# A two-layer graph network on one core: one tile of source rows in every fourth block as TensorE products in place of a gather

## The chip, the cores and the metric

The kernel runs on one NeuronCore of one Trainium2 chip. The metric is the device time of one execution in microseconds (us). TensorE, VectorE, ScalarE, GpSimd and SyncE appear in the profile as PE, DVE, ACT, POOL and SP; PEld is TensorE's weight load.

## The reference, cut to what matters

A graph has 6250 nodes of 128 features and 200,000 edges, sorted by destination. Two layers run one after the other, each with a residual sum.

```python
h = relu(layernorm(x))                        # layer 0: attention over edges, 8 heads of 16
z = h @ W;  el, er = z . attn_l, z . attn_r   # per node and head
e = leaky_relu(el[src] + er[dst])
a = exp(e - segment_max(e, dst)[dst])
x = x + segment_sum(z[src] * a, dst) / segment_sum(a, dst) + bias
h = relu(layernorm(x))                        # layer 1: messages weighted by a small network
s, v = h[:, :32] @ W_up_s, h[:, 32:] @ W_up_v # 128 numbers a node: the table of layer 1
w0, w1, w2, w3 = silu(silu(edge8 @ A1 + b1) @ A2 + b2) @ A3
m = [s[src]*y_s*w0, (v[src].y_v)*w3, s[src]*y_v*w1, v[src]*y_s*w2]   # 256 numbers an edge
x = x + (segment_sum(m, dst) / 10) @ W_out
```

Both layers need, for every edge, the row of its source node: 136 numbers in layer 0, 128 in layer 1.

## The kernel before, in words

**Tiles and blocks.** 128 edges make a tile, 1563 tiles in all, and 16 tiles (`KB`) make a block, 98 blocks (`NB`). As the edges are sorted, a block's destinations lie in a window of 128 nodes. `one_hot` (line 1146) compares a tile's destinations with `iota` and gives a 128x128 matrix `s`; the sum over edges is then a TensorE product of `s` and the messages, into `p_u`. `finish` (line 1154) joins the windows of adjacent blocks, and every second block completes one tile of 128 nodes, of which there are 50 (`NX`).

**Source rows.** Each layer first has its table in DRAM, `t0` or `t1`, one row a node. `gather` (line 831) issues one indirect DMA on GpSimd for each tile of 128 edges and brings 128 rows into one slot of the block's buffer `z` (name `g`). `z_pool` has five such buffers, so GpSimd can run ahead of the arithmetic. GpSimd does nothing else in the loops. In every third block (`by_row`, line 1106: 31 blocks) the last tile is left out of the gathers. `rows_by_row` (line 1117) has SyncE read 128 row addresses into registers and issue 128 row DMAs in place of it; `rows_until` spreads them over three blocks; `filled` (line 1142) has ScalarE copy the tile `r` into `z`.

**Layer 0** (the loop at line 1415) computes logits, maxima and weights of a block, multiplies and sums. For each complete node tile `node_x`, `node_d`, `node_h`, `node_t`, `node_s` compute the new x and the rows `sv` of the table of layer 1, and `node_out` (line 1343) has SyncE write `sv` to `t1` and to `t1z`. The second table lets the first 24 gathers (`NE`) of layer 1 begin before the last three node tiles (`NL`) are known: their rows are zero there, and `late_ends` and `late_rows` add them as f32 TensorE products with `sv_late`. All x lie in SBUF in `x_all`, 50 x 128 x 4 bytes a partition, from layer 0 until layer 1 ends.

**Layer 1** (the loop at line 1709) goes by steps of four tiles, four steps a block. At a block's first step `take_rows(b + 2)` asks for the gathers of the block after the next, and `edge_rows(b + 2)` has SyncE load edge data `ft` and `yb`. Each step then has, in this order: a quarter of the next block's `network` (TensorE products into `p_h`, ScalarE activations), `tensor_weights` of the next step (`p_w`), `messages` of this step (seven VectorE operations that read `z` and write `mj`), `one_hot` of the next step, `finish` and `node1` where a window is complete, and `sums1` (TensorE, from `mj` into `p_u`). `node1` (line 1625) transposes the sums, has ScalarE copy them, multiplies by `wout` and adds to x; `node_out1` has SyncE write the result one block later. PSUM's eight banks are full: two each of `p_h`, `p_w`, `p_u`, one `p_n`, and one `p_i` (called `held`), which keeps a copy of `iota` and the edge vectors `yp` of three blocks.

**Order.** TensorE, VectorE, ScalarE and SyncE run strictly in the written order (`manual_schedule`), and semaphores between engines follow from the tiles that are read and written. GpSimd's queue holds the gathers in their order. An engine that waits holds up all that is queued behind it on that engine.

A check of the data at the start picks this program or a general one that makes no use of windows. The profiled execution took this one.

Of the kernel before, what the change touches and what calls it, by code (L numbers as in the profile page):

```python
# [18 lines left out]
P = 128  # L19
# [10 lines left out]
KB = 16  # L30
# [711 lines left out]
def tile_even_edges(  # L742
# [88 lines left out]
    def gather(to, table, tiles, width, first=0):  # L831
        for k, t in enumerate(tiles, first):
            nc.gpsimd.indirect_dma_start(  # L833
                out=to[:, k, :width], out_offset=None, in_=table,
                in_offset=bass.IndirectOffsetOnAxis(ap=src_col[:, t : t + 1], axis=0))
        return to
# [171 lines left out]
def even_edges(tc, v):  # L1008
# [8 lines left out]
    with ExitStack() as ctx:  # L1017
        z_pool = ctx.enter_context(tc.tile_pool(name="fz", bufs=5))
        const = ctx.enter_context(tc.tile_pool(name="fconst", bufs=1))
        s_pool = ctx.enter_context(tc.tile_pool(name="fs", bufs=16))  # L1020
        row_pool = ctx.enter_context(tc.tile_pool(name="frow", bufs=3))
        of_l0 = ctx.enter_context(ExitStack())
        l0c = of_l0.enter_context(tc.tile_pool(name="l0c", bufs=1))
# [15 lines left out]
        x_all = const.tile([P, NX, P], F32, name="fx_all")  # L1039
# [3 lines left out]
        identb = l0c.tile([P, P], BF, name="fidentb")  # L1043
        nc.vector.tensor_copy(identb, ident)
# [50 lines left out]
        a3p = const.tile([P, 2, P], F32, name="fa3p")  # L1095
        nc.sync.dma_start(a3p, v["a3p"])
# [4 lines left out]
        wout = const.tile([P, 2, P], F32, name="fwout")  # L1101
        nc.sync.dma_start(wout, v["wout"])
# [43 lines left out]
        def one_hot(t, m, iota=iota):  # L1146

            s = s_pool.tile([P, 4, P], F32, name="s")
            nc.vector.tensor_tensor(s[:, :m], iota[:, None, :].to_broadcast([P, m, P]),  # L1149
                                    dloc[:, t : t + m].unsqueeze(2).to_broadcast([P, m, P]),  # L1150
                                    OP.is_equal)
            return s

        def finish(b, p_u, width, carry, agg, pool):
# [10 lines left out]
            return carry, agg  # L1165

# [5 lines left out]
        with tc.manual_schedule(engines=in_order), \  # L1172
# [116 lines left out]

            def node_rows(i, n):  # L1290
                nc.sync.dma_start(x_all[:, i : i + n, :],
                                  xp[i * P : (i + n) * P].rearrange("(j p) f -> p j f", p=P))

            def with_bias(i, n):
                x_i = x_all[:, i : i + n, :]
                nc.vector.tensor_add(x_i, x_i, bias_b[:, None, :].to_broadcast([P, n, F]))

            def node_x(u):
                i, n, agg = u["i"], u["n"], u["agg"]
                x_i = x_all[:, i : i + n, :]  # L1300
# [14 lines left out]
            def node_h(u):  # L1315
                i, n = u["i"], u["n"]
                rs, mr = normal(l0n, u["mv"], u["rs"], n, f"n{n}")
                xn = u["xn"] = l0n.tile([P, 2, P], F32, name="xn")
                nc.scalar.activation(xn[:, 0, :], x_all[:, i, :], AF.Identity, bias=mr[:, 0, :],
                                     scale=rs[:, 0, :])  # L1320
                if n == 2:
                    nc.vector.tensor_scalar(xn[:, 1, :], x_all[:, i + 1, :], u["mv"][:, 1, 0:1],
                                            rs[:, 1, :], op0=OP.subtract, op1=OP.mult)
# [19 lines left out]
            def node_out(u):  # L1343
                i, n, sv = u["i"], u["n"], u["sv"]
                first = i * P - W0
                for table in (t1, t1z) if i < LATE else (t1,):
                    if i == 0:
                        nc.sync.dma_start(table[: P - W0, :], sv[W0:, 0, :])
                    else:
                        nc.sync.dma_start(  # L1350
                            table[first : first + n * P].rearrange("(j p) f -> p j f", p=P), sv)

# [62 lines left out]
            for g in range(NG - 3):  # L1415
# [17 lines left out]
                maxima(c)  # L1433
                ends_of(n2, 1)
# [30 lines left out]
                ends_of(n2, 3)  # L1465
                for n in nodes:
                    node_s(n)
                late = nodes
                if b4:
                    sums(b4, 8)  # L1470
                if g == NG - 4:
# [16 lines left out]
            maxima(c3)  # L1488
            neighbours(c4, c5, c3)
# [26 lines left out]
            (u,) = ended(c4, st)  # L1516
            weighted(c2, 0)
# [22 lines left out]
        with tc.manual_schedule(engines=in_order), \  # L1540
                tc.tile_pool(name="l1", bufs=3) as l1, \
                tc.tile_pool(name="l1n", bufs=2) as l1n, \
                tc.tile_pool(name="l1_ps", bufs=2, space=PSUM) as l1_ps:

# [8 lines left out]
            def network(b, step):  # L1553
# [7 lines left out]
                if step == 3 or 2 * q0 + 8 >= KT[b] and second:  # L1561
                    c["yp"] = held[:, P + b % 3 * KB * 3 : P + (b % 3 + 1) * KB * 3].rearrange(
# [61 lines left out]

            def node1(i, agg):
                x_i = x_all[:, i, :]
                p_n = l1_ps.tile([P, 4, P], F32, name="p_n", bufs=1)
# [3 lines left out]
                nc.scalar.copy(m_t, p_n[:, :2])  # L1631
                for q in range(2):
                    nc.tensor.matmul(p_n[:, 2, :], m_t[:, q, :], wout[:, q, :], start=q == 0, stop=q == 1)
                nc.vector.scalar_tensor_tensor(x_i, p_n[:, 2, :], POST, x_i, op0=OP.mult, op1=OP.add)
                return i

            def node_out1(i):
                x_i = x_all[:, i, :]
                if i == 0:
                    nc.sync.dma_start(out[: P - W0, :], x_all[W0:, 0, :])  # L1640
# [5 lines left out]
            iota_p = held[:, :P]  # L1646
# [25 lines left out]
            def late_rows(t):  # L1672
                if t < NE:
                    z, k0, oh = blk[t // KB]["z"], t % KB, late_ends.of.pop(t)
                    p_n = l1_ps.tile([P, 4, P], F32, name="p_n", bufs=1)
                    for k in range(4):
                        for j in range(NL):
                            nc.tensor.matmul(p_n[:, k, :], oh[:, j, k, :], sv_late[:, j, :],
                                             start=j == 0, stop=j == NL - 1)
                    z = z[:, k0 : k0 + 4, :P]  # L1680
                    nc.vector.tensor_add(z, z, p_n)
# [6 lines left out]
            def take_rows(b):  # L1688
# [3 lines left out]
                elif b < NB:  # L1692
                    blk[b]["z"] = gathered(t1, range(b * KB, b * KB + KT[b] - (b in by_row)), P)

            rows, rows_until.n, late = rows_by_row(1, t1, P), 0, []
# [9 lines left out]
            us[0]["s"] = one_hot(0, us[0]["m"], iota_p)  # L1705
# [3 lines left out]
            for i, u in enumerate(us):  # L1709
                b, k0, m = u["b"], u["k0"], u["m"]  # L1710
                if k0 == 0:
                    take_rows(b + 2)
                    filled(1, b, blk[b]["z"], P)
                    edge_rows(b + 2)
                if k0 == 4:
# [8 lines left out]
                messages(u)  # L1724
                late_rows(4 * (i + 1))
                if i + 1 < NU:
                    n = us[i + 1]
                    n["s"] = one_hot(n["b"] * KB + n["k0"], n["m"], iota_p)
# [18 lines left out]
            p_n = l1_ps.tile([P, 4, P], F32, name="p_n", bufs=1)  # L1747
# [11 lines left out]
            x_i = x_all[:, NX - 2 :, :]  # L1759
# [140 lines left out]
```

## Time and profile before

| | us |
|---|---|
| median of 3 runs | 6222.33 (6202.72 to 6229.55) |
| the profiled execution's own time | 3867.0 |
| its span, first to last instruction | 3865.1 |
| layer 0 to layer 1, about | 1967 from the start |
| busy: GpSimd, TensorE, VectorE, ScalarE | 2900.2, 2825.6, 2237.5, 1403.0 |
| GpSimd gathers of lines 833 and 899 | 3064, a little under 1 us busy each |
| TensorE clock granted, layer 0 and layer 1 | 0.65, 0.97 |
| SyncE row DMAs | 7936, 0.5 KB each |

The runs are without a profile and take much longer than the execution that was profiled. Every duration below is from that one execution. In the lines of the profile, "L833" is a line of the kernel, "out<-in" are tile names, and the part after the bar gives the idle time of the engine just before and what ended it.

### The profile page before, as it was taken

The page shows a single profiled execution, that of the slowest core. Times are in us where ns is not written, and L with a number is a line of the kernel's source. Part 1 is how long each engine was busy: PE and PEld are TensorE (multiplying, and loading weights), DVE is VectorE, ACT ScalarE, POOL GpSimd, SP SyncE. Part 2 cuts the span into 40 slices and gives each one's busy share as a digit, 9 for nine tenths or more (in the row PEclk, how much of TensorE's full clock was granted, in tenths as well). Part 3 has the DMA queues.
Part 4 walks back from the last instruction along what each step waited for, and adds up shares of the span by engine and source line. Part 5 has one row for each costly group of instructions (what it writes and reads, how often), then busy time and mean ns, then how long its engine had stood idle before and what let it go on. Part 6 is the DMA issues. An engine that isn't in the chain of part 4 may idle for free. (4 is left out here: it accounts for less than half of the span.)

```text
span 3865.1 us, 62861 instructions
## 1 busy us (share of the span) xinstructions
PE 2825.6 (73%) x14836; PEld 2380.3 (62%) x14836; DVE 2237.5 (58%) x5485; ACT 1403.0 (36%) x3625; POOL 2900.2 (75%) x3074
## 2 busy tenths in 40 slices
PE   4666566666666666666688888888887788888777
PEld 3666566666566656656576666666665666666655
DVE  6555444444444444444457777777766666666666
ACT  3333322232323233322324444444444444444443
POOL 6777777777777777777777777777777777777776
PEclk7676666666666666666689999999999999999999
DMA  6222222222222222222222222222222222222221
GB/s 176 60 64 62 65 64 62 65 64 63 63 64 63 64 62 65 62 64 62 62 60 62 62 62 62 62 63 62 61 63 62 62 62 62 62 61 62 61 61 50
DMA packets 192048, 250.91 MB, mean 65 GB/s; under 512 B 78768, under 2 KB 141872, under 8 KB 191664
## 3 DMA queue, kind: packets, MB, share of 16 engines
q0 software_dynamic: 98048, 207.21, 22.6%
q1 hardware_dynamic: 93184, 39.50, 3.9%
q8 instruction: 120, 1.97, 0.2%
q14 instruction: 264, 2.16, 0.2%
q10 hardware_dynamic: 432, 0.08, 0.0%
HBM read 232.98 MB, written 13.25 MB: 64 GB/s over the span
## 5 line engine op out<-in xcount | busy, mean ns | idle before, releaser
L833 POOL DMA_INDIRECT g<-ft,fsrc x3024 | 2857.7, 945 | 934.4 <-issue 859.1
L1622 PE MATMUL p_u<-mj,s 128*128 128x256 f32 x3126 | 793.6, 398 | 211.2 <-DVE mj L1614 209.8
L1622 PEld LDWEIGHTS p_u<-mj,s 128*128 128x128 f32 x3126 | 591.1, 196 | 379.4 <-DVE mj L1614 303.3
L1286 PE MATMUL p_u<-g,s 128*128 128x136 f32 x3062 | 588.1, 372 | 1.0 <-DVE g L1281 0.4
L1286 PEld LDWEIGHTS p_u<-g,s 128*128 128x128 f32 x3062 | 563.2, 276 | 1.7 <-DVE g L1281 1.6
L1589 ACT ACTIVATE p_w<-p_w,yb 128x64 f32<-128x64 f32 x1563 | 450.3, 288 | 120.5 <-PE p_w L1585 78.8
L1605 DVE TENSOR_TENSOR vy<-g,p_i 128x384 f32<-128x384 f32 x387 | 213.0, 550 | 364.6 <-DMA g<-ft,fsrc 258.1
L1585 PE MATMUL p_w<-fa3p,h 128*128 128x256 f32 x1564 | 412.3, 387 | 0.0
L1203 PE MATMUL p_d<-fident,s 128*128 128x128 f32 x1563 | 370.6, 400 | 0.9 <-DVE s L1149 0.9
L1585 PEld LDWEIGHTS p_w<-fa3p,h 128*128 128x128 f32 x1564 | 289.3, 195 | 117.9 <-issue 51.9
L1228 DVE TENSOR_TENSOR e_s<-g,p_n 128x128 f32<-128x128 f32 x96 | 27.5, 286 | 554.6 <-DMA g<-ft,fsrc 498.1
L1570 ACT ACTIVATE h<-p_h,fb 128x512 f32<-128x512 f32 x196 | 134.7, 687 | 580.2 <-PE p_h L1568 580.2
L1203 PEld LDWEIGHTS p_d<-fident,s 128*128 128x128 f32 x1563 | 300.7, 218 | 11.6 <-DVE s L1149 1.1
L1196 ACT COPY mk<-p_m 128x385 f32<-128x385 f32 (+1 forms) x99 | 47.7, 482 | 701.4 <-PE p_m L1193 693.6
L1281 DVE TENSOR_TENSOR g<-g,pe 128x1024 f32<-128x1024 f32 x193 | 225.5, 1209 | 127.3 <-ACT g L1272 127.3
L1205 ACT CAST d<-p_d 128x512 bf16<-128x512 f32 x391 | 228.2, 586 | 180.4 <-PE p_d L1203 137.2
L1231 PE MATMUL pe<-fident,e_s 128*128 128x128 f32 x98 | 37.7, 384 | 329.9 <-DVE e_s L1229 329.9
L1149 DVE TENSOR_TENSOR s<-p_n,fdloc 128x512 f32<-128x512 f32 x391 | 266.1, 682 | 7.2 <-ACT sv L1341 3.4
L1149 DVE TENSOR_TENSOR s<-p_i,fdloc 128x512 f32<-128x512 f32 x391 | 266.4, 681 | 3.8 <-ACT p_i L1564 3.8
L1568 PE MATMUL p_h<-ft,fa1p 128*128 128x128 f32 x1568 | 215.4, 282 | 67.7 <-DMA ft<-in_e_f_dram 67.7
L1568 PEld LDWEIGHTS p_h<-ft,fa1p 128*128 128x128 f32 x1568 | 209.2, 196 | 88.6 <-issue 72.4
L1575 ACT ACTIVATE h<-p_h,fb 128x512 f32<-128x512 f32 x196 | 134.7, 687 | 304.4 <-PE p_h L1572 304.4
(213 smaller groups left out, 3345.6 us busy)
## 6 DMA issues: line engine op xcount, KB each, us to landing
r<-ft SPq DMA_DIRECT2D x3968, 0.5 KB
r<-ft SPq DMA_DIRECT2D x3968, 0.5 KB
g<-ft,fsrc POOLq DMA_INDIRECT x3024
ft<-in_e_f_dram SPq DMA_DIRECT2D x98, 64.0 KB
yb<-in_e_y_dram SPq DMA_DIRECT2D x98, 32.0 KB
fx_all<-in_e_xp_dram SPq DMA_DIRECT2D x48, 64.0 KB
out_dram<-fx_all SPq DMA_DIRECT2D x47, 64.0 KB
ft<-sv SPq DMA_DIRECT2D x46, 64.0 KB
```

What stands on the lines that cost most here:

```text
L833: nc.gpsimd.indirect_dma_start(out=to[:, k, :width], out_offset=None, in_=table, in_offset=bass.IndirectOffsetOnAxis(ap=src_col[:, t : t + ...
L1149: nc.vector.tensor_tensor(s[:, :m], iota[:, None, :].to_broadcast([P, m, P]), dloc[:, t : t + m].unsqueeze(2).to_broadcast([P, m, P]), OP. ...
L1203: nc.tensor.transpose(p_d[:, k, :], c["s"][q][:, k, :], ident)
L1205: nc.scalar.copy(d[:, :m], p_d[:, :m])
L1281: nc.vector.tensor_mul(zh, zh, p_a[:, k0 : k0 + m].unsqueeze(3).to_broadcast([P, m, H, D]))
L1286: nc.tensor.matmul(c["p_u"][:, :ZW], c["s"][k // 4][:, k % 4, :], c["z"][:, k, :], start=c["o"] + k == 0, stop=c["o"] + k == KT[c["b"]] - 1)
L1568: nc.tensor.matmul(p_h[:, q, :], a1p[:, q0 + q, :], c["ft"], start=True, stop=True)
L1570: nc.scalar.activation(c["h1"], p_h, AF.Silu, bias=b1)
L1585: nc.tensor.matmul(w[:, k : k + n].rearrange("p k a u -> p (k a u)"), c["h2"][q // 4][:, q % 4, :], a3p[:, :n].rearrange("p k f -> p (k f) ...
L1589: nc.scalar.activation(w[:, k, ::2, :], w[:, k, ::2, :], AF.Copy, scale=c["yb"][:, k0 + k, 0:1])
L1605: nc.vector.tensor_mul(vy, v_n, y_p)
L1622: nc.tensor.matmul(blk[b]["p_u"][:, :MW], u["s"][:, k, :], u["mj"][:, k, :], start=k0 + k == 0, stop=k0 + k == KT[b] - 1)
```

## The change

It concerns layer 1 and what layer 0 leaves behind for it.

- **Dense tiles.** In blocks 10, 14, ..., 90 (`dense1`, 21 blocks) tile 14 of 16 (`KD`) is not gathered. Its rows are made on TensorE: the table lies in SBUF as `t1s`, 50 node tiles in three bf16 parts whose sum is the f32 value. The node tiles are dealt into three ranges of 17 (`NR`). `dense_ends` spreads the edges' source numbers over the partitions with one f32 product and compares them with node numbers, which gives 17 one-hot matrices in bf16; `dense_rows` multiplies each with the three ranges' node tiles at once, 3 x 128 columns, for each of the three parts; `dense_taken` picks for each edge the range that it belongs to and writes the row into `z`. The steps of block b - 1 and of block b carry these (`dense_step`).
- **Parts.** In layer 0 `parts` splits each `sv` by two casts and two subtractions, and ScalarE's queue writes the parts to DRAM (`t1b`). Layer 1 loads them, six node tiles a block in its first eight blocks (`table_tiles`). The last three node tiles are split in SBUF.
- **x in DRAM.** `x_all` is gone. Layer 0 loads each node tile's x into a small buffer and ScalarE's queue writes the new x to `x1`; layer 1 loads it again (`node_rows1`).
- **Room.** `a3p` and `wout` are loaded at the start of layer 1; `one_hot` has a pool of 16 buffers in layer 0 and one of 5 in layer 1; `p_n` moves into the free half of the bank `held`, whose `yp` are now those of two blocks; its old bank becomes `p_x`, for `late_rows` and the dense tiles.

```diff
     def gather(to, table, tiles, width, first=0):
-        for k, t in enumerate(tiles, first):
+        for t in tiles:
+            k = first + t - tiles[0]
...
+        NR = -(-NX // 3)
+        KD = KB - 2
+        order = sorted(range(NR), key=lambda k: (k > 0, 2 * NR + k < NX, k))
+        half = (NR + 1) // 2
+        dense1 = set(range(10, NB - 4, 4))
...
+        def in_three(to, of, rest):
+            nc.vector.tensor_copy(to[:, :, 0, :], of)
+            nc.vector.tensor_sub(rest, of, to[:, :, 0, :])
+            nc.vector.tensor_copy(to[:, :, 1, :], rest)
+            nc.vector.tensor_sub(to[:, :, 2, :], rest, to[:, :, 1, :])
...
             def node_rows(i, n):
-                nc.sync.dma_start(x_all[:, i : i + n, :],
-                                  xp[i * P : (i + n) * P].rearrange("(j p) f -> p j f", p=P))
+                x_i = x_of[i] = l0n.tile([P, n, P], F32, name=f"x{n}", bufs=5 if n == 1 else 1)
+                nc.sync.dma_start(x_i, xp[i * P : (i + n) * P].rearrange("(j p) f -> p j f", p=P))
...
+                nc.scalar.dma_start(x1[i : i + n].rearrange("j p f -> p j f"), x_of.pop(i))
+
+            def parts(u):
+                i, n = u["i"], u["n"]
+                if i < LATE:
+                    u["parts"] = l0n.tile([P, 1, 3, P], BF, name="parts")
+                    in_three(u["parts"], u["sv"], l0n.tile([P, 1, P], F32, name="rest", bufs=1))
+
+            def parts_out(u):
+                if "parts" in u:
+                    nc.scalar.dma_start(t1b[u["i"]], u["parts"][:, 0])
...
+            def node_rows1(i, n=1):
+                x_i = x_of[i] = l1n.tile([P, n, P], F32, name=f"x{n}", bufs=4 if n == 1 else 1)
+                nc.sync.dma_start(x_i, x1[i : i + n].rearrange("j p f -> p j f"))
+
             def node1(i, agg):
-                x_i = x_all[:, i, :]
-                p_n = l1_ps.tile([P, 4, P], F32, name="p_n", bufs=1)
+                x_i = x_of[i][:, 0, :]
...
-            iota_p = held[:, :P]
+            iota_p, p_n = held[:, :P], held[:, 2 * P :].rearrange("p (j f) -> p j f", f=P)
...
+            def table_tiles(b):
+                i = 6 * b
+                if i < LATE:
+                    n = min(6, LATE - i)
+                    nc.sync.dma_start(t1s[:, i : i + n], t1b[i : i + n].rearrange("j p s f -> p j s f"))
+
+            def dense_ends(b):
+                p_x = blk[b]["p_x"] = l1_ps.tile([P, 4, P], F32, name="p_x", bufs=1)
+                nc.tensor.matmul(p_x[:, 3, :], key[:, b : b + 1].to_broadcast([P, P]), ident,
+                                 start=True, stop=True)
+                oh = blk[b]["oh"] = l1d.tile([P, NR, P], BF, name="ohs")
+                for k, n in ((0, half), (half, NR - half)):
+                    nc.vector.tensor_tensor(
+                        oh[:, k : k + n], p_x[:, 3:4, :].to_broadcast([P, n, P]),
+                        place_r[:, k : k + n].unsqueeze(2).to_broadcast([P, n, P]), OP.is_equal)
+
+            def dense_rows(b, k0, n):
+                c = blk[b]
+                for k in range(k0, min(k0 + n, NR)):
+                    i = order[k]
+                    m = len(range(i, NX, NR))
+                    for s in range(3):
+                        nc.tensor.matmul(c["p_x"][:, :m, :], c["oh"][:, k, :], t1s[:, i::NR, s, :],
+                                         start=k == 0 and s == 0, stop=k == NR - 1 and s == 2)
+
+            def dense_taken(b):
+                c = blk[b]
+                z = c["z"][:, KD, :P]
+                nc.vector.tensor_scalar(z, c["p_x"][:, 0, :], part[:, b, 0:1], None, op0=OP.mult)
+                for r in (1, 2):
+                    nc.vector.scalar_tensor_tensor(z, c["p_x"][:, r, :], part[:, b, r : r + 1], z,
+                                                   op0=OP.mult, op1=OP.add)
+
+            def dense_step(b, q):
+                if b + 1 in dense1:
+                    if q == 1:
+                        dense_ends(b + 1)
+                    elif q > 1:
+                        dense_rows(b + 1, (q - 2) * 4, 4)
+                if b in dense1:
+                    dense_rows(b, 8 + 3 * q, 3)
+                    if q == 2:
+                        dense_taken(b)
...
                     edge_rows(b + 2)
+                    if b % 2 == 0:
+                        node_rows1(b // 2, 1 if b < NB - 2 else 2)
+                    table_tiles(b)
...
                 messages(u)
+                if i == 26:
+                    in_three(t1s[:, LATE:], sv_late, rest)
+                dense_step(b, k0 // 4)
                 late_rows(4 * (i + 1))
```

## The prediction

> **What bounds the kernel now.** I read the page first, its line of engines, then its costliest group.
>
> ```profile
> span 3865.1 us, 62861 instructions
> PE 2825.6 (73%) x14836; PEld 2380.3 (62%) x14836; DVE 2237.5 (58%) x5485; ACT 1403.0 (36%) x3625; POOL 2900.2 (75%) x3074
> L833 POOL DMA_INDIRECT g<-ft,fsrc x3024 | 2857.7, 945 | 934.4 <-issue 859.1
> ```
>
> No engine looks full. But GpSimd's idle time is almost all "issue" (859.1 of 934.4 us): it waits for nothing that the profile shows. One gather is 945 ns busy plus some 300 ns of issue. Next, busy time by stretches for that line alone (columns: stretch, length, busy and count, TensorE clock, DMA share, GB/s).
>
> ```profile
> 500.00:1000.00 500.00, 378.00 (x401) 0.63 0.28 64
> 2500.00:3000.00 500.00, 377.98 (x401) 0.97 0.24 62
> ```
>
> It is the same count, 401 in 500 us, in the first layer and in the second: a pitch of 1.247 us that never breaks. GpSimd makes 3064 gathers in all (3024, and 40 in the smaller groups); 3064 x 1.247 = 3821 us of 3865. The two layers are one queue of gathers, and everything else follows it. Then the waits between 2100 and 3850 us, to see how closely the second layer follows (columns: total us, times, longest).
>
> ```profile
> DVE vy L1605 <- DMA g<-ft,fsrc: 257.1, 158, 3.7
> PE p_h L1568 <- DMA ft<-in_e_f_dram: 62.3, 25, 4.9
> ```
>
> VectorE waits for gathered rows, which is the proof from the consumer's side. The second line is a warning: TensorE also waits for edge data that SyncE loads. So I read SyncE's queue in order of time and VectorE's beside it.
>
> ```profile
> 2035.10 0.37 SPq L1549 DMA_DIRECT2D ft<-in_e_f_dram  x1
> ...
> 2383.53 0.37 SPq L1549 DMA_DIRECT2D ft<-in_e_f_dram  x1
> ```
>
> Between these two loads lie 19 blocks: 18.34 us a block, with SyncE issuing row after row and hardly waiting. GpSimd needs 15.67 gathers a block (one tile in every third block is SyncE's), 19.53 us. SyncE is therefore only 1.2 us a block from being a bound.
>
> ```profile
> 2032.06 0.55 DVE L1605 TENSOR_TENSOR vy<-g,p_i 128x384 f32<-128x384 f32 x1 [1.56 <-ACT p_i L1564]
> ...
> 2065.35 0.56 DVE L1605 TENSOR_TENSOR vy<-g,p_i 128x384 f32<-128x384 f32 x1 [1.20 <-ACT p_i L1564]
> ```
>
> These are the fourth steps of two blocks, two apart, at the start of the layer, while arithmetic is behind the gathers: 33.3 us for two blocks, 16.65 each. That is the fastest pace of the arithmetic that the trace shows. The order of pressure in the second layer is thus gathers 19.53, SyncE 18.34, arithmetic 16.65 us a block.
>
> **What the Trainium skill says.** "DMA: Bandwidth & Descriptors", section "SWDGE vs HWDGE vs iDMA": for a GpSimd DMA a GpSimd core computes each descriptor in software. That agrees with 945 ns for any 128 rows, while the DMA engines are 28% busy. "TensorE: Matmul & The Clock Gate", section "Back-to-back issue gap": a warm product of N columns takes about N/2.4 + 2.5 ns. Eight records of 128x256 f32 in the second layer take 1.89 us, so (1.89 - 0.38)/7 = 0.216 us each: twice 256 columns at that rate. The trace has no stream of bf16 products of 384 columns; by the page they are 0.162 us each. "SBUF — State Buffer", section "Who interferes with whom": a VectorE copy or cast can hold the port pair that GpSimd needs. Here 33 multiply-type VectorE operations of line 951 ran among the first 16 gathers and the gathers kept a median of 944 ns, with one of 1092.
>
> **The change, part by part.**
>
> *Removed: gathers.* Blocks 10, 14, ..., 90 are 21 blocks, each with one tile of 128 rows fewer. 21 x 1.247 = **26.2 us** off GpSimd's queue, directly on the path.
>
> *Added, TensorE.* A dense block takes 17 row groups x 3 parts = 51 bf16 products of up to 384 columns (the last group has 256) and one f32 product. Low bound 51 x 0.162 = 8.3 us; high bound 51 x 0.451 = 23.0 us, by the only bf16 row of that size (128x385, line 1193, 451 ns when alone). I take 8.5: they come in runs of 9 or 12, in a layer whose clock is 0.97.
>
> *Added, VectorE.* Two comparisons of 1152 and 1024 elements from PSUM: by line 1281 (1024 elements, 1209 ns) 1.35 + 1.2 us. Three small operations of 128 elements, 0.29 each. Sum 3.4 us a dense block.
>
> *Do they fit?* In four blocks gathers now need 4 x 19.53 - 1.25 = 76.9 us; arithmetic needed 66.6. If nothing overlaps, 66.6 + 8.5 + 3.4 = 78.5; TensorE has 195.8 us of waits for `mj` in which the products can run, about half the addition, so some 72.5. I cost it at nothing, covered by the 10.3 us between 66.6 and 76.9. Gathers run up to four blocks ahead (five buffers), so two slow blocks do not stall them.
>
> *Moved: the transposes' bank.* The output product `p_n` now shares a bank with `iota_p` and `yp`. Line 1564 already waits for the comparisons of line 1149 (16.8 us, 21 times), so I expect the two transposes to wait for one comparison, and the message operations after them: up to 2 us for each of 48 nodes, in every second block. Inside the same cover; what is queued behind is `sums1` on TensorE.
>
> *Added, SyncE.* 49 loads of x and 8 of the table, 57 x 0.45 us = 26 us over 98 blocks, 0.24 a block in the long run: 18.34 becomes 18.6, gathers now need 19.2. Hidden, by 0.6 us a block. Each stands ahead of row loads. `a3p` and `wout` move to the layer's start: 0.9 us ahead of the first edge loads.
>
> *Added, first layer.* Per node VectorE two casts and two subtractions, about 1.0 us (128x128 subtraction near line 1309, 295 ns); ScalarE issues 97 DMAs at 0.45 us. VectorE waits 481.8 us for gathers between 300 and 1900 us, 6 us a block: free. Casts could hold up gathers: nothing to 94 x 0.2 = 19 us; I take 0, by line 951. The loop setup of ranges, some 6 us once, is also inside that wait. At the end of the layer 24 gathers from `t1z` bridge 30 us; the last table write is issued at 1962.15 and the first `t1` gather runs at 1967.4, so up to about 3 us of delay is free, and an ACT issue of 0.45 us fits.
>
> *Sum against the profiled execution.* 3867.0 - 26.2 = 3840.8 us, that is -0.68%; with the casts' bound -0.2%.
>
> **The runs shown are not that execution.** Their median, 6222.33, is 1.61 times 3867.0. No row says where the other 2355 us lie. I read it as longer gathers: 2355 / 3064 = 0.77 us each, a pitch of 2.02, for gathers are what everything waits on. Then 21 x 2.02 = 42 us go, again -0.68%: **6180 us**. If the difference is fixed time, only 26 go: 6196, -0.42%. About 0.5% is what a measurement of this kernel can tell from no change.
>
> **Rivals.**
>
> *The gain is real but too small to tell* (fixed extra time, or casts that hold up gathers): 6196 to 6210. For it: nothing in the trace shows a 2 us gather as the rule. Against: 2.4 ms of fixed time would be odd, since the execution's own time is 2 us over its span.
>
> *Nothing happens.* The program has a second branch for uneven edges, which the change does not touch. If the runs took it, 6222. The profile did not, and the data decide the branch.
>
> *SyncE is the bound.* If in the runs 7936 row loads fill the time, each takes 0.78 us and 57 more loads add 45 us: 6267, +0.7%. For it: 18.34 against 19.53. Against: between 2700 and 3865 us VectorE waits for gathers, not for `ft`.
>
> *Slower: the products do not hide.* Place: the step after `messages`, where `sums1` queues behind them on TensorE. If weight loads (118 ns for bf16, line 1214) do not overlap, 51 x 0.28 = 14.3, plus 3.4 on VectorE: (66.6 + 17.7)/4 = 21.1 us a block against 19.53, over 84 blocks +130 us, 3.4%: about 6430. It decides from 10.3 us of unhidden work a dense block. For it: TensorE is already 81% busy here. Against: f32 streams show weight loads hidden.
>
> **How the numbers follow.** Forecast 0.50, small gain 0.18, nothing 0.10, SyncE 0.10, slower products 0.10, a larger gain 0.02. Faster by over 0.5%: 0.46 of the forecast, the larger gain and 0.05 of the small one: 0.53. Within: 0.04 + 0.13 + 0.10 + 0.03 = 0.30. Slower: 0.17. The range goes from 6150 (the forecast less 0.5%, the spread of the three runs) to 6260, which takes in nothing and most of SyncE, and leaves out the slower products.
>
> **What would show it.** Right: 21 fewer gathers, the 1.247 us pitch unbroken to the end, VectorE still waiting for `g`, a span near 3839, products at about 0.16 us, `ft` waits somewhat up. Wrong: gathers waiting for VectorE in the second layer (buffers not freed), which is arithmetic as the bound; `ft` or `x` waits growing through the layer, which is SyncE; gathers over 945 ns in the first layer, which is the casts.

## The result, and the profile after

The changed kernel takes 6446.55 us (median of four runs, 6440.24 to 6466.43) beside 6219.98 us for the kernel before, a ratio of 1.0373 (95% interval 1.034 to 1.0406): 227 us slower, where 42 us less were forecast. One thing has to be known for every number below: the kernel before takes 3872 us in one session on the chips and 6220 to 6314 us in the seven others, one chip having been seen in both, so each ratio here is to the kernel before in the same session, the "quick" one or a "long" one. The result above is from a long session; the profile of before was of the quick kind. The text ahead of the prediction calls the runs unprofiled; that is not what sets the two apart, for the profiled execution of the changed kernel, 6449.9 us, is itself one of its four runs.

The page of after, the lines that answer to those of before, and the new group of products:

```profile
span 6448.1 us, 65601 instructions
PE 3219.5 (50%) x15949; PEld 2632.4 (41%) x15949; DVE 2354.9 (37%) x5805; ACT 1395.3 (22%) x3625; POOL 2878.6 (45%) x3053
L834 POOL DMA_INDIRECT g<-ft,fsrc x3003 | 2836.1, 944 | 3457.3 <-issue 1420.6
L1780 PE MATMUL p_x<-t1s,ohs 128*128 128x384 bf16 x1071 | 228.6, 368 | 268.0 <-DVE ohs L1770 251.4
```

Exactly 21 gathers are gone (3024 to 3003 in this group), and one still takes 944 ns. But GpSimd now stands idle for 3457 us, and only 1421 of them are put down to issue; some 2870 issues of 300 ns would be 860 us, so part of these is longer pauses too. The gathers by stretches, the same two as of before (busy and count, TensorE clock, DMA share, GB/s):

```profile
500.00:1000.00 500.00, 227.08 (x241) 0.59 0.18 40
2500.00:3000.00 500.00, 235.50 (x250) 0.60 0.19 42
```

There were 401 in each, but in a quick session. The nearest thing to before in a long session is `e12_tiny` (below), whose first layer is that of before:

```profile
500.00:1000.00 500.00, 237.91 (x253) 0.61 0.17 40
2500.00:3000.00 500.00, 241.22 (x257) 0.60 0.17 41
```

So most of the fall is the session's, and the change's part in layer 0 is 253 to 241 and 257 to 250. GpSimd is not the bound in either, so something holds it. Three waits of the changed kernel between 300 and 3000 us, all in the first layer:

```profile
POOL g L834 <- PE p_d L1239: 487.8, 25, 23.6
DVE e_s L1264 <- ACT g L1141: 483.7, 18, 33.5
ACT g L1141 <- DMA r<-ft: 466.7, 23, 40.4
```

Read upwards: ScalarE's copy of a row-loaded tile (line 1141) waits up to 40 us for the rows `r`, VectorE waits for that copy, and GpSimd waits for TensorE, in whose order the sums stand that give a buffer back. In the same view of `e12_tiny` the first is 442.6 us, the second 231.9 and the third 254.3, so it is the last two that have grown. The rows are late, and the next view is SyncE's own queue in the same stretch:

```profile
SPq L1127 <- DMA ft1b<-parts: 275.1, 29, 15.8
SPq L1127 <- DMA fx<-x: 17.0, 11, 2.7
```

Line 1127 loads one row of the old table. It shares no data with the write of the parts (`ft1b`) or of x (`fx`), and yet it waits 275 us for the first to land. `e12_tiny` has no such line. And in the second layer, between 3600 and 6300 us:

```profile
POOL g L834 <- DVE mj L1680: 761.0, 54, 20.6
```

GpSimd waits for messages, that is for arithmetic to free buffers. In a long session the second layer is not bound by gathers, with the change or without it: `e8_aside`, whose second layer is that of before, has 724.8 us of the same wait.

### The profile page after: what moved, and what is told of

The parts are those of the page before. It is cut to its first block, busy times and chain, and to the rows that moved or that the text cites. A ratio compares the mean times of both kernels' runs of the same rounds, so it can differ in the third digit from the quotient of the medians.

```text
span 6448.1 us, 65601 instructions
## 1 busy us (share of the span) xinstructions
PE 3219.5 (50%) x15949; PEld 2632.4 (41%) x15949; DVE 2354.9 (37%) x5805; ACT 1395.3 (22%) x3625; POOL 2878.6 (45%) x3053
## 5 line engine op out<-in xcount | busy, mean ns | idle before, releaser
L1688 PE MATMUL p_u<-mj,s 128*128 128x256 f32 x3126 | 874.5, 429 | 427.8 <-DVE mj L1680 371.8
L1688 PEld LDWEIGHTS p_u<-mj,s 128*128 128x128 f32 x3126 | 655.7, 216 | 585.9 <-DVE mj L1680 415.1
L1322 PE MATMUL p_u<-g,s 128*128 128x136 f32 x3062 | 636.0, 390 | 47.6 <-issue 47.6
L1322 PEld LDWEIGHTS p_u<-g,s 128*128 128x128 f32 x3062 | 606.0, 293 | 44.7 <-issue 44.7
L1673 DVE TENSOR_TENSOR p_w<-g,p_w 128x128 f32<-128x128 f32 x387 | 113.3, 293 | 894.2 <-ACT p_w L1655 784.9
L1780 PE MATMUL p_x<-t1s,ohs 128*128 128x384 bf16 x1071 | 228.6, 368 | 268.0 <-DVE ohs L1770 251.4
L1239 PE MATMUL p_d<-fident,s 128*128 128x128 f32 x1563 | 352.3, 383 | 10.3 <-issue 7.7
L1638 PE MATMUL p_h<-h,fa2p 128*128 128x512 f32 x392 | 229.5, 670 | 194.8 <-ACT h L1636 159.7
L1250 PEld LDWEIGHTS <-d 128*128 128x128 bf16 x1563 | 103.4, 116 | 508.7 <-ACT d L1241 320.7
```

The lines of the kernel that those rows point to most:

```text
L1239: nc.tensor.transpose(p_d[:, k, :], c["s"][q][:, k, :], ident)
L1322: nc.tensor.matmul(c["p_u"][:, :ZW], c["s"][k // 4][:, k % 4, :], c["z"][:, k, :], start=c["o"] + k == 0, stop=c["o"] + k == KT[c["b"]] - 1)
L1638: nc.tensor.matmul(p_h.rearrange("p q e -> p (q e)"), a2p, c["h1"].rearrange("p q e -> p (q e)"), start=True, stop=True)
L1688: nc.tensor.matmul(blk[b]["p_u"][:, :MW], u["s"][:, k, :], u["mj"][:, k, :], start=k0 + k == 0, stop=k0 + k == KT[b] - 1)
L1780: nc.tensor.matmul(c["p_x"][:, :m, :], c["oh"][:, k, :], t1s[:, i::NR, s, :], start=k == 0 and s == 0, stop=k == NR - 1 and s == 2)
```

## The experiments

Theories: **C**, the sum of the prediction. **Q**, the two DMAs that ScalarE issues per node in layer 0 hold SyncE's queue of row loads. **V**, the casts or the writes cost time by themselves. **P**, the products do not hide on TensorE. **R**, the number of instructions sets the time. **S**, SyncE's row loads are the bound. **W**, the bytes of ScalarE's two writes crowd the DMA engines. The expectations name a few more (G, the loss lies in the second layer; I and D) where they need them.

### Quick session: four kernels

The kernel before, unchanged (`e1_same`).

> The kernel before, unchanged, to have a second profile of it. The profile of it that was read was 3867 us, its runs 6220; the changed kernel's profile and its runs are both near 6450. Theory R (records): in every run the recording of instructions holds the engines up, so that time goes by the number of recorded instructions; the new profile should be near 6220 us, and the count of recorded instructions, DMA packets and semaphore updates per us should be as even through both layers as in the changed kernel, near 10 instructions per us. Theory C (cover): the first profile is the true one and the products of the dense tiles do not hide in the second layer; the profile is near 3867 again. Theory S (SyncE): row loads are slow in the runs; the profile is near 6220, with row loads of about 0.75 us against 0.43, and GpSimd waiting in both layers.

3872.11 us. C's time: the condition of the profile of before is a real one. All experiments of this section come from one session on one chip.

No tile by rows (`e2_no_rows`):

```
-        by_row = [b for b in range(3, NB - 2) if b % 3 == 0]
+        by_row = []
```

> The kernel before with no tile given to SyncE: the 62 tiles of by_row are gathered too, so 7936 row loads with their register moves go and 62 gathers come. R: some 16,200 fewer of 62,861 instructions at 0.099 us each: about 4600 us, bounded from below by 3126 gathers x 1.247 = 3900. S: the row loads are gone, so the gathers bound it, 3900 to 3950 us. C, if the first profile stood for the runs: 62 x 1.247 = 77 us slower than before, 6300.

3949.33 us, 1.0200 (1.0183 to 1.0217): +77.4 us, and 62 more gathers x 1.247 = 77.3. In the quick session gathers are the bound, to the microsecond.

Products of 16 columns in place of 128 for each range (`e3_narrow`), the other columns of the dense rows set to zero, otherwise the changed kernel:

```
-  nc.tensor.matmul(c["p_x"][:, :m, :], c["oh"][:, k, :], t1s[:, i::NR, s, :], ...
+  nc.tensor.matmul(c["p_x"][:, :m, :16], c["oh"][:, k, :], t1s[:, i::NR, s, :16], ...
```

> The changed kernel with products of 3 x 16 columns in place of 3 x 128: as many products, an eighth of the columns; 112 of the 128 numbers of a dense tile's rows are zeros. C: most of TensorE's added time goes (51 x 0.16 us to about 51 x 0.06 a dense block), so the loss of 227 us falls to about 80 or less, near 6300 us. R: the same number of instructions (21 more on VectorE), so 6447 us, within 10. S: 6447 too.

4059.53 us, 1.0492 (1.0475 to 1.051). The loss is there although the products' width is almost gone, so P does not explain it here; the changed kernel itself was not timed in the quick session. Its profile shows where it lies. The gathers by stretches:

```profile
500.00:1000.00 500.00, 338.51 (x358) 0.64 0.23 60
2500.00:3000.00 500.00, 378.14 (x400) 0.97 0.23 64
```

The second layer keeps the old pace, the first has lost 11% of it. SyncE's queue between 300 and 1950 us, of this kernel:

```profile
SPq L1127 <- DMA ft1b<-parts: 281.5, 38, 9.9
SPq L1127 <- DMA fx<-x: 20.6, 12, 2.3
SPq L1388 <- ACT d L1241: 2.8, 8, 0.4
```

and of the kernel before:

```profile
SPq L1350 <- ACT sv L1341: 149.0, 13, 38.1
SPq L1350 <- ACT g L1144: 25.1, 5, 13.8
```

Before, SyncE's largest waits were for ScalarE's `sv` at the table write: that was its spare time. It is used up, and 302 us of new waits stand at the row loads. As SyncE falls behind, its table writes come late too, and ScalarE waits for them, which before it did for 4.2 us in all:

```profile
ACT sv L1379 <- DMA ft1z<-sv: 301.7, 26, 16.5
```

So the two queues hold up each other, and SyncE waits for hardly anything else (2.8 us): it has taken the gathers' place as the bound of layer 0. One wait of SyncE, in ScalarE's timeline (start, us):

```profile
996.02 0.33 ACTq L1400 DMA_DIRECT2D ft1b<-parts  x1
```

Each DMA raises a semaphore (a counter that engines wait on) as it lands. The trace's records name it, and the record of a row load names the same number as what it waits for. SyncE's rows before this write raise 104, 105, ... 109, 101 in turn, the last issued at 990.8 us; the next in turn is 103, which is the number of ScalarE's write. SyncE's next row, also 103, is issued at 998.3 us, 7.4 us later instead of 0.32, and 2.2 us after the write's issue. The node's next write of the parts, issued at 1029.9 with number 107, has the same after it: the next row with 107 is issued 2.2 us later. It is the rule: after 45 of the 47 writes of the parts SyncE stands still directly before the next row of that number, which is issued 1.6 to 2.4 us after the write; in the profile of the changed kernel it is 45 of 47 too, after 1.6 to 2.2 us. The DMAs of the two queues take their numbers in written order from one set of eight, and a row load waits for the DMA that had its number before. No run gave the two queues separate numbers; this mechanism is read from the records. ScalarE reaches its write late, behind casts that wait for TensorE, and SyncE, ahead of it, stops.

1176 products of 8 columns that nothing reads, in layer 1 of the kernel before (`e4_tiny`; `tiny` is a bf16 matrix of 128x128):

```
+                for _ in range(3):
+                    nc.tensor.matmul(p_h[:, 0, :8], tiny, tiny[:, :8], start=True, stop=True)
```

> The kernel before with three bf16 products of 8 columns ahead of each quarter of the network in the second layer, 1176 in all, whose results are overwritten: 2352 more instructions (weight loads and products) and about 1176 x 0.06 = 70 us of TensorE in a layer where it waits 300 us. R: 2352 x 0.099 = 233 us more, about 6450 us, almost the loss of the change. C and S: hidden, 6220 us, at most 30 more.

3872.36 us, 1.0001 (0.9992 to 1.001). Instructions with no one waiting for them cost nothing here; R falls for the quick session.

### Long session: the DMAs moved, and alone

The changed kernel again (`e5_after`).

> The changed kernel itself, beside the kernel before. Theory Q (the two DMAs that ScalarE issues per node in the first layer, the write of x and the write of the three parts, hold up SyncE's queue of row loads, the rows come late, and GpSimd waits for buffers): the loss lies in the first layer and the narrow kernel lost 187 us there less its gain in the second, so about 4060 us, ratio 1.04 to 1.055, POOL about 360 gathers in 500 us of the first layer, SyncE's row loads waiting some 280 us for the write of the parts. Theory P (products of full width do not hide): later than the narrow kernel by much of 21 x 8.3 us, 4150 to 4240. Theory C (the sum of the prediction): 3841.

6534.14 us beside 6299.1, 1.0384 (1.0362 to 1.0405). It ran in a long session and repeats the result. All three times that I had expected were for a quick one; Q's sign, SyncE's wait for the parts, is there with 247.6 us where some 280 were expected.

Both writes on SyncE (`e6_both_sync`), the parts one block later, so that SyncE does not wait for the casts (the core of the edit; the new loop stands ahead of `node_out`):

```
-                nc.scalar.dma_start(x1[i : i + n].rearrange("j p f -> p j f"), x_of.pop(i))
+                nc.sync.dma_start(x1[i : i + n].rearrange("j p f -> p j f"), x_of.pop(i))
-                    nc.scalar.dma_start(t1b[u["i"]], u["parts"][:, 0])
+                    nc.sync.dma_start(t1b[u["i"]], u["parts"][:, 0])
+                for n in cast:
+                    parts_out(n)
-                for n in late:
-                    parts_out(n)
-                late = nodes
+                cast, late = late, nodes
```

> The changed kernel with both DMAs issued by SyncE instead of ScalarE, the write of the parts one block later, in front of the next node's write. Everything else, casts and products too, is as changed. Theory Q: the loss of the first layer goes, what is left is the gain of 21 gathers less the waits of the second layer: 3840 to 3860 us, ratio 0.992 to 0.997, L0 to L1 at about 1967 us as before. Theory V (the three casts on VectorE, four instructions a node, make the first layer late): as the changed kernel, about 4060. Theory W (the bytes of the two writes crowd the DMA engines): as the changed kernel, about 4060.

6400.88 us, 1.0169 (1.0149 to 1.019): 133 of the 235 us are taken back. The same bytes and the same casts are still there, so neither W nor V explains these 133. Only the write of the parts moved (`e7_parts_sync`):

> The changed kernel with only the write of the parts issued by SyncE, one block later; ScalarE still issues the write of x. Theory Q, by the waits of the narrow kernel's first layer (281 us for the parts, 21 us for x): most of the loss goes, 3845 to 3890 us; above the kernel with both moved by the part of x. Theories V and W: about 4060.

6502.7 us, 1.0331 (1.0312 to 1.035): 31 us only. I had expected most of the loss to go, because x had only 20 us of the waits. SyncE's queue of this kernel, 300 to 3000 us, says why:

```profile
SPq L1127 <- DMA fx<-x: 298.3, 28, 18.6
```

The write of x has taken the place of the other: with either left on ScalarE's queue, SyncE stops. With both moved neither line is there, and the longest wait of a row load is 1.5 us, for other rows. (VectorE's casts now wait for the moved write of the parts, 327.6 us in this stretch, but layer 0 is as short as without them; see the table.) Then ScalarE's two DMAs alone in layer 0 of the kernel before (`e8_aside`), with nothing else of the change:

```
+                nc.scalar.dma_start(aside[0, i : i + n].rearrange("j p f -> p j f"),
+                                    x_all[:, i : i + n, :])
...
+            def aside_out(u):
+                if u["i"] < LATE:
+                    nc.scalar.dma_start(aside[1, u["i"]], u["sv"][:, 0])
```

> The kernel before, and in its first layer alone ScalarE issues two DMAs per node that nothing reads: x (64 KB) to a DRAM table at the place where the change writes x, and the node's table rows in f32 (64 KB, the change's parts are 96 KB) at the place where the change writes the parts. No casts, no products, no change in the second layer. Theory Q: the loss comes back without the rest of the change: 3872 plus 150 to 200 us, ratio 1.04 to 1.055. Theory V: 3872. Theory W: between 3872 and 4060. Theories G and P (it lies in the second layer): 3872.

6465.83 us, 1.0263 (1.0237 to 1.029), +167 us, and the same wait under another name:

```profile
SPq L1131 <- DMA faside<-sv: 293.5, 28, 16.6
SPq L1131 <- DMA faside<-fx_all: 20.4, 12, 2.6
```

So the DMAs on ScalarE's queue do it, without a cast and without a product. In long sessions Q holds, and V does not for layer 0. In the quick session no run took the DMAs out or put them in alone: there Q rests on the waits of `e3_narrow`.

### Long session: what is left

> The changed kernel, ScalarE's two DMAs per node and all else included, but with no tile's rows loaded one by one: the list of such tiles is empty in both layers, and GpSimd gathers those 62 tiles too. The kernel before took 3872 us on one chip and 6299 on another; so it matters on which this runs. Theory Q (ScalarE's DMAs harm only by holding SyncE's queue of row loads) with S (on the chip of 6299 that queue, 7936 row loads at about 0.75 us, is itself the bound): without row loads neither is left, and GpSimd's gathers are the bound on either chip: 3949 (no rows, no change) - 21 x 1.247 = 3923 us, up to 3950. Theory V (casts and writes cost time by themselves): 3923 + 187 = 4110. Theory R (on the chip of 6299 the number of instructions sets the time, 10.1 per us): about 49100 instructions, 4860 us there.

`e9_after_no_rows` (the changed kernel with `by_row = []`): 5679.7 us beside 6311.02, 0.900 (0.8985 to 0.9015). Neither S (3923) nor R (4860).

> The changed kernel with both writes issued by SyncE (the parts one block later) and with row loads for every sixth block's tile instead of every third's, so about 31 tiles more are gathered and 3968 row loads fewer issued. Theories Q and S: SyncE needs at most 4200 x 0.75 = 3150 us even on the chip where the kernel before took 6299, so GpSimd is the bound on either: 3845 + 31 x 1.247 = 3884 us, up to 3950. Theory R: about 57000 instructions, 5650 us on the chip of 6299. Theory V: 4070.

`e10_half_rows` (both writes moved, `b % 6`): 6133.21 us, 0.9728 (0.971 to 0.9746), far from 3884 and from R's 5650. S falls: row loads are dear in a long session, but with half of them gone only 294 us went (`e11_both_sync`, of the same session, has them all), so SyncE's queue of rows does not set the time alone.

> The changed kernel with both writes issued by SyncE, the parts one block later: the kernel that ran at 6401 beside 6299. On the chip where the kernel before takes 3872, by theory Q: 3840 to 3860 (ratio 0.992 to 0.997); by V or W: about 4060. On a chip where it takes 6299: 6401 again.

`e11_both_sync`: 6427.69 us, 1.018 (1.0163 to 1.0197), a long session again.

> The kernel before with three products of 8 columns ahead of each quarter of the network in the second layer, 1176 in all, that nothing reads. On the chip where the kernel before takes 3872 it made no difference (3872.4). On the chip of 6299: theory R: 1176 products, 2352 instructions with their weight loads, at 10.1 per us: +230 us; theories S and Q: within 20 us of 6299.

`e12_tiny`: 6376.3 us, 1.0097 (1.0079 to 1.0115). The products that cost nothing in the quick session cost 65 us here, 65 / 2253 more instructions = 0.029 us each, or 0.055 for each of the 1176 products: less than R's price, but not nothing. Whether it is a price of instructions or of TensorE's time this run can't tell. Its waits, 300 to 3000 us and 3600 to 6300 us:

```profile
ACT d L1207 <- remote: 687.7, 110, 13.3
```

```profile
POOL g L833 <- DVE mj L1618: 749.7, 55, 18.3
```

The first is a pause of ScalarE at a plain cast of TensorE's result for which the view has no releaser ("remote"); the same view of before has none. Such pauses run through the long sessions' traces, on ScalarE above all. In reading them one has to know that these traces hold fewer records of semaphores, some 37,000 in the changed kernel's against 85,000 in that of before, so what ended a wait is less sure there. The second shows that arithmetic holds the gathers in layer 1 without dense blocks too.

No dense block, all else as with both writes moved (`e13_no_dense`, `dense1 = set()`), beside the kernel with them (`e14_both_sync`):

> The changed kernel with both writes issued by SyncE (the parts one block later) and with no dense block: every tile of the second layer is gathered (or loaded by rows) as before; the casts, the two writes, and the loads of the table and of x in the second layer stay. On the chips where the kernel before takes 6300: theory I (every instruction added to the second layer costs there about 0.028 us, as 2353 instructions that nothing waits for cost 65 us): without 1071 products and their weight loads the second layer loses 60 to 70 us against the kernel with both writes moved, ratio to before 1.004 to 1.010. Theory D (the loss left in the second layer is from the loads, or from the transposes' bank): stays at 1.017. On the chip of 3872, theory C: no gathers saved, 3872 to 3880 us, 26 us above the kernel with both writes moved.

> The changed kernel with both writes issued by SyncE, the parts one block later, beside the last one. On the chips of 6300: 1.017 to 1.018 again. On the chip of 3872: theory Q with C 3840 to 3860 us; theories V and W about 4060.

6349.83 us, 1.0053 (1.0036 to 1.007), and 6420.78, 1.0173 (1.0149 to 1.0197), as theory I expected. The dense blocks, which were to save 26 us, cost 71. Are they TensorE's time or the count? Narrow products with both writes moved (`e15_narrow_sync`; the same instructions, the dense rows' other columns zero):

> The changed kernel with both writes issued by SyncE, the parts one block later, and with products of 3 x 16 columns instead of 3 x 128 (the other columns of the dense rows are set to zero): as many instructions, some 185 us less of TensorE's time. On the chips where the kernel before takes 6300: theory I (the cost is per instruction): 1.015 to 1.018, as with full products; theory P (TensorE's time of the products is not hidden there): 1.005 to 1.008, as without dense blocks. On the chip of 3872: theory Q with C: 3840 to 3860 us, where the same kernel with both writes on ScalarE took 4060; theories V and W: about 4060.

6390.55 us, 1.014 (1.0105 to 1.0176). The interval leaves out P's 1.005 to 1.008 and holds the value with full products: most of it is not the products' width. The price agrees with `e12_tiny`, 71 us / 2283 instructions = 0.031, but that is no proof of a price per instruction: the narrow kernel keeps the comparisons and sums on VectorE too, which the prediction put at 3.4 us a dense block, 71 us for 21. And the profile of the changed kernel has a place for the loss, 3600 to 6300 us:

```profile
DVE ohs L1770 <- remote: 276.4, 20, 16.3
PE p_x L1780 <- DVE ohs L1770: 239.1, 20, 15.0
```

Each first comparison of a dense block (`ohs`) waits some 14 us, and the products wait for it. In `e14_both_sync` the comparison starts 14.2 to 16.2 us after the TensorE product that it reads has ended, in all 21 dense blocks; in `e3_narrow`, quick, 0.0. VectorE waits there for the semaphore that TensorE raises. In the first dense block the product ends at 3526.6 us; that semaphore has one record between 3527 and 3539 us and nine between 3542.1 and 3542.6, though TensorE ran products that raise it in between. At 3542.1 and 3542.2 ScalarE and VectorE start, both of which wait for it. So at these places the pauses are waits for raises of TensorE's semaphore that arrive late and in a bunch. The pauses are as long in `e15_narrow_sync` (286.3 us in all, against 289.4). Why the raises come late, and how much of the 71 us is this, stays open.

> The changed kernel with both writes issued by SyncE, the parts one block later. On the chip where the kernel before takes 3872: theory Q with C 3840 to 3860 us (ratio 0.992 to 0.997); theories V and W about 4060. On the chips of 6300: 1.017 again.

> The changed kernel with both writes issued by SyncE, the parts one block later. On the chip where the kernel before takes 3872: theory Q with C 3840 to 3860 us (ratio 0.992 to 0.997); theories V and W about 4060. On the chips of 6300: 1.017 again.

`e16_both_sync` gave 6328.04 us, 1.017 (1.0152 to 1.0188), and `e18_both_sync` 6331.35 us, 1.0157 (1.014 to 1.0174); both fell in long sessions. So the kernel with both writes moved was never timed in a quick one, and its forecast of 3840 to 3860 us there stays untested.

> The kernel before without row loads: all 62 tiles are gathered by GpSimd too; nothing of the change is in it. On the chip of 3872 it took 3949. On the chips of 6300 it is to be set beside the changed kernel without row loads (5680 us, 0.900 of before), which has ScalarE's two writes per node, the casts and the dense blocks in addition. Theory Q (the writes cost only by holding the row loads): only the dense blocks' 76 us lie between the two, so about 5590 to 5610 us (ratio 0.885 to 0.89). Theory V or W (casts or writes cost by themselves): 76 + 130 us between them, about 5470 us (0.867).

`e17_no_rows`: 5456.52 us beside 6237.27, 0.8749 (0.8733 to 0.8765), as a ratio between the two expectations. The stage table tells which layer holds the difference to `e9_after_no_rows`. I split each profile at the first `vy` that reads `g` (the second block of layer 1):

| kernel, session | to the first `vy` | from there |
|---|---|---|
| before, quick | 2015.7 | 1849.4 |
| `e3_narrow`, quick | 2232.5 | 1824.5 |
| `e12_tiny` (layer 0 as before), long | 3242.5 | 3150.0 |
| `e8_aside` (layer 1 as before), long | 3398.7 | 3070.1 |
| `e5_after`, long | 3377.0 | 3153.5 |
| `e7_parts_sync`, long | 3349.9 | 3144.1 |
| `e6_both_sync`, long | 3248.0 | 3151.0 |
| `e13_no_dense`, long | 3237.7 | 3075.4 |
| `e15_narrow_sync`, long | 3259.2 | 3137.8 |
| `e9_after_no_rows`, long | 2872.5 | 2792.2 |
| `e17_no_rows`, long | 2839.1 | 2615.7 |

The rows of long sessions are from five chips, and a profiled execution can be off its median: that of `e13_no_dense` is the shortest of five, 35 us under it. Long sessions have no profile of before; its layers stand in the rows of `e12_tiny` and `e8_aside`, and against these `e5_after` has 134 us more in layer 0 and 83 in layer 1, 218 of the 235 measured.

The last two stem from sessions in which the kernel before took 6311.02 and 6237.27. In shares of these, layer 0 is 0.455 in both: ScalarE's writes and the casts cost nothing measurable where no row loads stand behind them, as Q says. The difference is all in layer 1, 0.442 against 0.419, more than the 76 us that I had put there; why the dense blocks cost more without row loads is open.

## Why the prediction was wrong, point by point

**"Added, first layer" failed.** It priced ScalarE's 97 DMAs at 0.45 us of ScalarE and called them free, because VectorE has waits there. It didn't ask who on SyncE waits for them to land. Layer 0 grew by 134 us in a long session (3377.0 against 3242.5), and with both DMAs moved all but 6 of these are gone (3248.0). In the quick session it grew by 217 (2232.5 against 2015.7, with narrow products); how much of that is the DMAs no run separates. "What bounds" had a warning in hand, for the second layer: SyncE 1.2 us a block from a bound.

**"The runs shown are not that execution" failed.** I read the extra 2355 us as longer gathers, which carried the bound over to the runs. Gathers are as long as ever (944 ns); the time lies in waits and pauses around them. The 26 us of "Removed: gathers", scaled to 42, were therefore not on the path: GpSimd waits for `mj` there, which the prediction had named as a sign of being wrong; but the old second layer has that wait in a long session too.

**"Do they fit?" held only where its cover exists.** In the quick session layer 1 of the narrow kernel is 24.9 us shorter (1849.4 to 1824.5), where 21 x 1.247 = 26.2 were forecast. But VectorE's waits for `g` after the start of layer 1 fell from 257.1 us to 22.5, so little cover seems left; with full products it was not run. The shared bank was priced well: the transposes wait for the comparison 40 times there, 1.4 us at most. In long sessions the gathers are not the bound, so the cover of 10.3 us a dense block is absent, and the dense blocks cost 71 us.

**Sizes.** The bf16 products were priced right. In the changed kernel's profile they follow each other, from start to start, at a median of 0.163 us, the 0.162 that the prediction worked out from the Trainium skill's "TensorE: Matmul & The Clock Gate", section "Back-to-back issue gap". Their mean of busy time, 228.6 / 1071 = 0.213 us, is higher in part because 161 of the 954 steps within a run of products take 0.320 us; the TensorE clock was 0.79 to 0.82 in that layer. The casts hardly lengthened the gathers (947 ns in `e3_narrow`, 945 before, 6 us in all), so taking 0 of their 0 to 19 us was near, though only 20 of the 33 operations of line 951 ran among the first 16 gathers. SyncE's added loads are 26 / 98 = 0.26 us a block and not 0.24; the 18.6 is right.

**The rivals.** None named the cause. "The products do not hide" had the sign and nearly the time (6430 against 6447), by luck: with narrow products the loss remains, and most of it lies in layer 0. "SyncE is the bound" had the engine, but looked for added loads, all in layer 1, and not for a stop of the queue.

**The sum after the fact.** In one long session the change costs 235 us (`e5_after`). ScalarE's DMAs are 133 of it (`e5_after` less `e6_both_sync`), the dense blocks 71 (`e14_both_sync` less `e13_no_dense`). The casts, the writes on SyncE and the 57 loads of layer 1 are 36 (`e13_no_dense` less before), which no run splits. Together 240, from two sessions.

**A version that beats both.** In long sessions it is the kernel before without row loads, 0.8749, and of the changed kernels `e9_after_no_rows`, 0.900. In the quick session the same edit to the kernel before gives 1.0200. None was shown to beat both kernels in both.

## What to carry to other kernels

A DMA that is put on another engine's queue is not priced by that engine's issue time alone: look in the records for which later DMAs wait for it to land, above all when it is issued late by an engine that runs behind a queue with little room. Two writes that both stop a queue hide each other in a profile; moving the one with all the waits moves the waits to the other. Compare profiles of the same condition: most of what sets the two pages of this text apart is not the change. And when the runs take 1.6 times the profiled execution, the bound of the profile must not be carried over to them: forecast both conditions, and give the range both.

## What the runs showed of the hardware

- A row load of SyncE came 7.4 us after the one before it, because of a DMA of ScalarE that it shares nothing with but the number of a semaphore; after 45 of 47 such writes the row with the number followed 1.6 to 2.4 us after the write's issue (`e3_narrow`).
- The same kernel took 3872 us in one session and 6220 to 6314 us in others, on one chip both. In the long sessions engines pause, ScalarE by up to 19 us at a time in layer 1 of the changed kernel; in the 21 dense blocks of `e14_both_sync` the pause ends as raises of TensorE's semaphore arrive, 14 to 16 us after the product. What delays them is open.
- 1176 products whose results nothing reads cost 65 us in a long session and nothing in the quick one.
- 128x384 bf16 products followed each other at a median of 0.163 us, in a layer with a mean clock of 0.79 to 0.82.
- Without row loads, 16468 instructions fewer, the kernel before takes 12.5% less in a long session (`e17_no_rows`) and 2.0% more in the quick one (`e2_no_rows`).
